# Edge softmax on one core: blocks taken from the fewest slots to the most, and a second turn that follows its block's first turn by two or three steps

## The chip, the core and the metric

The kernel runs on one core of a Trainium2 chip. The metric is the device time of one execution in microseconds (us). The unchanged kernel took 7273.15 us in the median of three runs (7250.3, 7273.15 and 7337.22 us).

## What is computed

A graph of 6250 nodes and 200,000 edges passes through four layers. Each layer adds its result to x after a layer normalisation and a ReLU. The change lies in the third layer, an edge softmax in which every edge has 256 logits and 256 messages:

```python
w_m = (efeat @ W_msg + b_msg).reshape(E, 16, 16)
w_a = (efeat @ W_attn + b_attn).reshape(E, 16, 16)
h_src = feat[src][:, :, None]
e1, e2 = w_m * h_src, w_a * h_src
seg_max = segment_max(e2, dst)
ex = exp(e2 - seg_max[dst])
attn = ex / segment_sum(ex, dst)[dst]
ft = segment_sum(e1 * attn, dst)
return ft.sum(axis=1)          # one row of 16 for each node
```

So a node's maximum over all of its edges has to be known before the first exponential of that node is taken.

## The kernel before

**Blocks, slots, groups.** The nodes are sorted by their number of edges and cut into 49 blocks of 128, one node on each partition. Block b has HELD[b] slots, one edge of each of its nodes in every slot. HELD falls from 64 for block 0 to 21 for block 48 and sums to 1611. Slots are worked on in groups of four (the last group of a block may be shorter). There are 421 groups: 16 in block 0, 12 in block 1, 11 in block 2, down to 6 in block 48.

**Two turns.** Each group is handled twice in `softmax_ranked`.

- The first turn takes the attention logits from TensorE (`logits`, matmuls of L1037 into the PSUM tile `pw`). VectorE multiplies them with the source node's features into `e2` (L1058) and takes a maximum for each partition into `tops` (L1060). After the last group of a block, `less` (L1064) is the negative maximum of the block.
- The second turn asks TensorE for the message logits (again L1037, another `pw` buffer). ScalarE takes exp(e2 + less) into half of the tile `both` (L1069). VectorE multiplies the message logits with the features (L1074) and with the exponentials into the other half (L1075). TensorE adds the group's slots up with identity matmuls into the PSUM tile `acc` (L1083), one of 512 columns for each slot. After the last group, ScalarE copies `acc` out (L1086), and VectorE divides and reduces (L1088 to L1092).

**Steps.** A loop over t writes out all of this by hand: the matmuls for step t+1, `first_take` for step t, the exponential for step t+1, `second_take` for step t and `second_sum` for step t-1. Two lists say which group is in its first turn (`ones`) and which in its second turn (`twos`). The blocks come in the order 0, 1, ..., 48, and `twos` is `ones` shifted by LAG:

```python
LAG = len(groups(0)) // 2 * 2 + 1            # 17
HS = LAG + 1 + len(groups(1)) + len(groups(2))   # 41
ones = [g for b in range(NT) for g in groups(b)]
twos = [None] * LAG + ones + [None]
```

So there are 438 steps: 17 with a first turn alone, 404 with both, 17 with a second turn alone. An odd shift puts the first and the second turn of a step into different halves of the partitions that hold the transposed attributes, and the matmuls of the two halves are issued alternately.

**What is loaded.** `load(b)` puts three kinds of work into the queue of POOL (GpSimd), which works in order. One indirect DMA brings the block's edge attributes (`attr`, L693, three buffers). One indirect DMA for every slot brings 16 features of the slot's 128 source nodes (`hs`, L1007, a tile for each group, HS buffers). A block's result goes out with another indirect DMA (`store`, L51). A tile `hs` is in use from its gather until L1074 of the group's second turn has read it. An `attr` tile is free again when `turn` has copied the block's last pair of groups out of it: ScalarE spreads the attributes (L1018, L1019), TensorE transposes them (L1022), ScalarE copies them to `turned` (L1024). The scheduler of the language orders the instructions within each engine's queue, and can place the attribute load of a block before or behind gathers of other blocks.

**Buffers that bear on the order.** `pw` has three PSUM buffers, `both` four, `e2` LAG + 2 = 19, `turned` LAG // 2 + 7 = 15, `tops` and `less` six, `acc` one.

Of the kernel before, what the change touches and what calls it, by code (L numbers as in the profile page):

```python
# [34 lines left out]
def at(ap):  # L35
    return bass.IndirectOffsetOnAxis(ap=ap, axis=0)
# [914 lines left out]
def softmax_ranked(tc, inp, S, R, dram, x, h):  # L951
# [4 lines left out]
    D, NT = R.D, R.NT  # L956
# [3 lines left out]
    with tc.tile_pool(name="f1", bufs=1) as f1, tc.tile_pool(name="f2", bufs=2) as f2, \  # L960
# [17 lines left out]
        def groups(b):  # L978
            return [(b, s0, min(4, HELD[b] - s0)) for s0 in range(0, HELD[b], 4)]

        def place(b, s0):

            return divmod(s0 + shift[b], 8)

        shift = [4 * (sum(len(groups(i)) for i in range(b)) % 2) for b in range(NT)]

        def chunks(b):
            return place(b, HELD[b] - 1)[0] + 1
# [4 lines left out]
        out = f1.tile([P, NT, D], F32, name="out")  # L993
        state = {}
        LAG = len(groups(0)) // 2 * 2 + 1
        HS = LAG + 1 + len(groups(1)) + len(groups(2))

        def load(b):
            n = HELD[b]
            attr = f2.tile([P, K, D], F32, name="attr", bufs=3)  # L1000
            R.block(attr[:, :n, :].rearrange("p k d -> p (k d)"), inp["edge_attr_16"], b)
            state["attr", b] = attr
            for _, s0, m in groups(b):
                hs = f2.tile([P, 4, D], F32, name="hs", bufs=HS)
                for k in range(m):
                    s = R.base[b] + s0 + k
                    nc.gpsimd.indirect_dma_start(out=hs[:, k, :], out_offset=None, in_=table, in_offset=at(R.src_i[:, s:s + 1]))  # L1007
                state["h", b, s0] = hs

        def turn(b, c):  # L1010

            n, attr, t = HELD[b], state["attr", b], wide[c % 2]
            s0 = 8 * c - shift[b]
            for q in range(2):
                i = [i for i in range(4) if 0 <= s0 + 2 * i + q < n]
                if i:
                    a, z = s0 + 2 * i[0] + q, s0 + 2 * i[-1] + q + 1
                    nc.scalar.copy(t[:, q, i[0]:i[-1] + 1, :D], attr[:, a:z:2, :])  # L1018
                    nc.scalar.copy(t[:, q, i[0]:i[-1] + 1, PAD], R.empty[:, R.base[b] + a:R.base[b] + z:2])  # L1019
            pt = fp.tile([P, 2, P], F32, name="pt")  # L1020
            for q in range(2):
                nc.tensor.transpose(pt[:, q, :], t[:, q].rearrange("p k w -> p (k w)"), S["ident"])  # L1022
            turned = f2.tile([P, 2, P], F32, name="turned", bufs=LAG // 2 + 7)
            nc.scalar.copy(turned, pt)  # L1024
            state["turned", b, c] = turned
# [23 lines left out]
        def ask(first, second):  # L1049
            asked = [(*what, k) for k, what in enumerate((first, second)) if what]  # L1050
            for (b, s0, _, k), pw in zip(asked, logits(*asked)):
                state["am"[k], b, s0] = pw

        def first_take(b, s0, m):
            e2 = f2.tile([P, 4, C], F32, name="e2", bufs=LAG + 2)
            if s0 == 0:
                state["tops", b] = f2.tile([P, K // 4], F32, name="tops", bufs=6)
            nc.vector.tensor_mul(four(e2[:, :m, :]), four(state.pop(("a", b, s0))[:, :m, :]), by_h(b, s0, m))  # L1058
            tops = state["tops", b]
            nc.vector.tensor_reduce(tops[:, s0 // 4:s0 // 4 + 1], e2[:, :m, :], axis=AX.XY, op=OP.max)  # L1060
            state["e2", b, s0] = e2
            if s0 + m == HELD[b]:
                less = f2.tile([P, 1], F32, name="less", bufs=6)
                nc.vector.tensor_reduce(less, tops[:, :s0 // 4 + 1], axis=AX.X, op=OP.max, negate=True)  # L1064
                state["less", b] = less

        def second_exp(b, s0, m):
            both = f2.tile([P, 4, 2 * C], F32, name="both", bufs=4)
            nc.scalar.activation(both[:, :m, :C], state.pop(("e2", b, s0))[:, :m, :], AF.Exp, bias=state["less", b])  # L1069
            state["both", b, s0] = both  # L1070

        def second_take(b, s0, m):
            both, pm = state["both", b, s0], state.pop(("m", b, s0))
            nc.vector.tensor_mul(four(pm[:, :m, :]), four(pm[:, :m, :]), by_h(b, s0, m))  # L1074
            nc.vector.tensor_mul(both[:, :m, C:], pm[:, :m, :], both[:, :m, :C])  # L1075

        def second_sum(b, s0, m):
            if s0 == 0:
                state["acc", b] = fp.tile([P, 2 * C], F32, name="acc")
            acc, both = state["acc", b], state.pop(("both", b, s0))  # L1080
            n = HELD[b]
            for k in range(m):
                nc.tensor.matmul(acc, S["ident"], both[:, k, :], start=s0 + k == 0, stop=s0 + k == n - 1)  # L1083
            if s0 + m == n:
                sums = f2.tile([P, 2 * C], F32, name="sums")
                nc.scalar.copy(sums, acc)  # L1086
                q = f2.tile([P, C], F32, name="q")
                nc.vector.tensor_scalar(q, sums[:, :C], 1.0e-30, None, op0=OP.max, op1=OP.min, accum_out=low[:, b:b + 1])  # L1088
                nc.vector.reciprocal(q, q)
                nc.vector.tensor_mul(q, sums[:, C:], q)  # L1090
                nc.vector.tensor_reduce(out[:, b, :], q.rearrange("p (i o) -> p o i", o=D), axis=AX.X, op=OP.add)
                nc.vector.tensor_scalar(out[:, b, :], out[:, b, :], R.some[:, b:b + 1], None, op0=OP.mult)  # L1092

        def store(b):
            by_node.store(ft, R.node_i[:, b:b + 1], out[:, b, :])

        ones = [g for b in range(NT) for g in groups(b)]
        twos = [None] * LAG + ones + [None]
        ones = ones + [None] * (LAG + 1)
        loaded = turned = stored = 0  # L1100
        todo = [(b, c) for b in range(NT) for c in range(chunks(b))]
        where = {bc: k for k, bc in enumerate(todo)}
        for t in range(-1, len(ones) - 1):
            now, late = (ones[t], twos[t]) if t >= 0 else (None, None)
            if ones[t + 1]:
                b, s0, _ = ones[t + 1]
                while loaded < min(b + 2, NT):
                    load(loaded)
                    loaded += 1
                    if loaded > 6:  # L1110
                        store(stored)
                        stored += 1
                while turned < min(where[b, place(b, s0)[0]] + 2, len(todo)):
                    turn(*todo[turned])
                    turned += 1
            ask(ones[t + 1], twos[t + 1])
            if now:
                first_take(*now)
            if twos[t + 1]:
                second_exp(*twos[t + 1])  # L1120
            if late:
                second_take(*late)
            if t >= 1 and twos[t - 1]:
                second_sum(*twos[t - 1])
        second_sum(*twos[len(ones) - 2])
        while stored < NT:
            store(stored)
            stored += 1
        by_node.done(R.cell)
    with tc.tile_pool(name="f3", bufs=1) as f3:  # L1130
# [276 lines left out]
def gnn(ctx: ExitStack, tc: tile.TileContext, inp, out):  # L1407
# [188 lines left out]
    with tc.If(odd == 0):  # L1596
        with tc.tile_pool(name="fast", bufs=1) as fast:
            dense = Dense(tc, inp, out, S, dram)
            ranked = Ranked(tc, inp, S, fast, dram)
            with tc.tile_pool(name="early", bufs=1) as early:  # L1600
                ranked.scatter()
                with tc.tile_pool(name="slots", bufs=1) as sl:
                    mean_of_edges(tc, inp, S, S["x"], S["h"], lambda b: dense.gather(sl, b))
                    dense.prepare(early)
                ranked.build(early)
                with tc.tile_pool(name="d2", bufs=2) as d2, tc.tile_pool(name="dp", bufs=3, space=PSUM) as dp, \
                        tc.tile_pool(name="dv", bufs=1, space=PSUM) as dv:
                    pieces = dense.build(d2, dp, dv)
                    rational_message(tc, inp, S, ranked, dram, S["x"], S["h"], lambda: next(pieces, None))
                    for _ in pieces:  # L1610
                        pass
            softmax_ranked(tc, inp, S, ranked, dram, S["x"], S["h"])
            dense.wrong = fast.tile([P, 1], F32, name="wrong")
            dense.convolve(S["x"], S["h"])
            ranked.vanishes(fast, dense.wrong, S["odd"])
# [24 lines left out]
```

## Time and profile before

| what | value |
|---|---|
| runs | 7250.3, 7273.15, 7337.22 us |
| profiled execution, its own time | 7443.48 us |
| its span, first to last instruction | 7441.7 us |
| share of the span in which PE, DVE, ACT, POOL are busy | 69%, 57%, 18%, 50% |
| granted clock of TensorE, mean | 0.85 |
| softmax stage: first attribute load to last `out` (L1092) | 3776 to 6777 us |

The profiled execution is 2.3% slower than the median of the runs. All times below are of that execution, and are counted from the start of its span.

A row of a group names the line, the engine, the operation, what it writes and reads, the number of instructions, then the busy time and the mean time of one, then the idle time of the engine just before them with what ended most of it. "remote" and "issue" are waits for which the profile names no instruction. In a table of windows each engine has its busy time and the number of its instructions in that stretch, and PEclk is the clock that TensorE was granted. In a timeline each row has the start, the time, the engine, the line and the tiles, and in brackets the idle time of the engine just before.

### The profile page before, as it was taken

The numbers are of one execution on the slowest core, as the hardware profiler recorded it, in microseconds if no ns is written. First come the engines' busy times: TensorE is split into PE (matmuls) and PEld (weight loads), VectorE is DVE, ScalarE is ACT, GpSimd is POOL, SyncE is SP. The second block draws the span as 40 slices with busy tenths as digits, with TensorE's granted clock in tenths as the row PEclk, the third lists the DMA queues.
The fourth block names the chain that finished last, engine by engine and source line by source line (L and its number), as shares of the span: only waits on it lengthen the run. The fifth ranks groups of instructions, "written<-read, shape, count | busy, mean of one in ns | idle before, by whom it ended". The sixth has DMA issues, their size and how long they took to land.

```text
span 7441.7 us, 69771 instructions
## 1 busy us (share of the span) xinstructions
PE 5142.0 (69%) x26293; PEld 2696.5 (36%) x26293; DVE 4245.6 (57%) x6282; ACT 1337.5 (18%) x2912; POOL 3693.8 (50%) x3729
## 2 busy tenths in 40 slices
PE   0002376767685686777724888888878888898999
PEld 0000144434443344444411334344333334343544
DVE  3753255645564565665523677677667767784211
ACT  0000022212221222222101222222222222220000
POOL 4657654654555555555355555555555555520000
PEclk9997688877787788888856888888888888899999
DMA  2411000000000000001010000000000000004843
GB/s 34 144 14 5 6 22 22 14 22 21 14 22 22 13 22 22 22 14 26 4 18 9 11 10 9 10 10 10 11 10 11 9 9 10 10 4 153 270 148 90
DMA packets 264161, 243.52 MB, mean 33 GB/s; under 512 B 128033, under 2 KB 249819, under 8 KB 260291
## 3 DMA queue, kind: packets, MB, share of 16 engines
q1 hardware_dynamic: 140630, 168.04, 7.8%
q0 software_dynamic: 123184, 70.93, 6.5%
q8 instruction: 209, 3.42, 0.2%
q14 instruction: 138, 1.13, 0.1%
HBM read 195.57 MB, written 43.14 MB: 32 GB/s over the span
## 4 chain that ended last, share of the span: by engine, by line
PE 38%; another core or an unknown queue 17%; issue 16%; POOL 12%; DVE 11%; DMA 2%; ACT 1%; SPq 0%; DVEq 0%; POOLq 0%; ACTq 0%
PE acc L905 18%; POOL hs L1007 9%; PE acc L1353 7%; PE acc L1083 6%; PE pa L1268 3%; PE pw L1037 2%; DVE e L1058 2%; DVE pw L1074 1%; DVE both L1075 1%; DVE ohc L898 1%; DVE st L893 1%; POOL raw L693 1%; POOL slots L1163 1%; DMA hs<-h,rk_src 1%
## 5 line engine op out<-in xcount | busy, mean ns | idle before, releaser
L853 POOL DMA_INDIRECT xi<-h,rk_src x1611 | 1748.7, 1085 | 1328.5 <-DVE den L870 831.7
L1007 POOL DMA_INDIRECT hs<-h,rk_src x1611 | 1521.0, 944 | 1091.1 <-DVE pw L1074 553.0
L905 PE MATMUL acc<-ohc,st 128*128 128x392 bf16 x9666 | 1849.3, 349 | 181.0 <-issue 136.4
L1083 PE MATMUL acc<-both,ident 128*128 128x512 f32 x3222 | 1690.2, 672 | 21.1 <-ACT sums L1086 11.9
L905 PEld LDWEIGHTS <-st 128*128 128x128 bf16 x9666 | 989.1, 103 | 930.3 <-issue 338.0
L1058 DVE TENSOR_TENSOR e<-pw,hs 128x1024 f32<-128x1024 f32 (+2 forms) x421 | 492.1, 1169 | 889.4 <-remote 666.1
L1083 PEld LDWEIGHTS acc<-both,ident 128*128 128x128 f32 x3222 | 651.0, 213 | 872.4 <-issue 851.0
L1037 PE MATMUL pw<-w,turned 18*128 18x256 f32 x6444 | 675.1, 449 | 397.6 <-DVE e L1058 361.7
L893 DVE TENSOR_TENSOR st<-ohx,s 128x1024 bf16<-128x1024 bf16 (+5 forms) x666 | 387.4, 636 | 798.7 <-remote 577.6
L1268 PE MATMUL pa<-oh,ol 128*128 128x98 bf16 x3136 | 372.6, 268 | 637.3 <-ACT adj L1271 329.5
L1069 ACT ACTIVATE both<-e,less 128x1024 f32<-128x1024 f32 (+2 forms) x421 | 467.5, 1111 | 1911.2 <-PE acc L1083 822.6
L1037 PEld LDWEIGHTS pw<-w,turned 18*128 18x128 f32 x6444 | 397.5, 205 | 677.6 <-DVE e L1058 408.6
L1271 ACT CAST adj<-pa 128x392 fp8e4<-128x392 f32 x784 | 347.2, 492 | 1626.8 <-remote 910.0
L898 DVE TENSOR_SCALAR ohc<-places,c 128x784 bf16<-128x784 f16 x1611 | 567.3, 417 | 0.0
L1268 PEld LDWEIGHTS <-ol 128*128 128x128 bf16 x3136 | 299.0, 117 | 726.7 <-issue 690.6
L1353 PE MATMUL acc<-adj,g 128*128 128x512 fp8e4 (+1 forms) x2548 | 540.0, 368 | 30.8 <-DVE g L1313 30.8
L1074 DVE TENSOR_TENSOR pw<-pw,hs 128x1024 f32<-128x1024 f32 (+2 forms) x421 | 495.9, 1178 | 75.7 <-PE pw L1037 30.3
L1075 DVE TENSOR_TENSOR both<-pw,both 128x1024 f32<-128x1024 f32 (+2 forms) x421 | 491.8, 1168 | 4.9
L1060 DVE TENSOR_REDUCE tops<-e 128x1 f32<-128x1024 f32 (+2 forms) x421 | 489.0, 1163 | 1.1
L1263 DVE TENSOR_TENSOR ol<-many,lot 128x2048 bf16<-128x2048 bf16 x196 | 238.3, 1216 | 290.2 <-remote 250.4
L1353 PEld LDWEIGHTS <-g 128*128 128x128 bf16 x2548 | 235.8, 98 | 316.4 <-issue 63.8
L890 ACT COPY ohx<-oha 128x1024 bf16<-128x1024 bf16 (+7 forms) x222 | 214.6, 967 | 544.5 <-DVE st L893 216.1
(257 smaller groups left out, 2584.6 us busy)
## 6 DMA issues: line engine op xcount, KB each, us to landing
adj<-adj SPq DMA_DIRECT2D x252, 448.0 KB
adj<-adj SPq DMA_DIRECT2D x24, 1568.0 KB
xi<-h,rk_src POOLq DMA_INDIRECT x1611
hs<-h,rk_src POOLq DMA_INDIRECT x1611
dis_row<-dis_d SPq DMA_DIRECT2D x1, 3136.0 KB
adj<-adj SPq DMA_DIRECT2D x21, 112.0 KB
rk_pairs<-both SPq DMA_DIRECT2D x1, 1562.5 KB
runs<-in_dst,row_i POOLq DMA_INDIRECT x49
```

The source lines that it names most:

```text
L853: nc.gpsimd.indirect_dma_start(out=xi[:, k, :], out_offset=None, in_=table, in_offset=at(R.src_i[:, s:s + 1]))
L898: nc.vector.tensor_scalar(ohc[:, j, :], places, c[:, s0 + j:s0 + j + 1], None, op0=OP.is_equal)
L905: nc.tensor.matmul(o, st[:, k, j].rearrange("p a d -> p (a d)"), ohc[:, j, half * CW // 2:(half + 1) * CW // 2], start=s == 0 and k == 0, ...
L1007: nc.gpsimd.indirect_dma_start(out=hs[:, k, :], out_offset=None, in_=table, in_offset=at(R.src_i[:, s:s + 1]))
L1037: nc.tensor.matmul(pw[:, k, :], state["turned", b, c][r:r + ROWS, q, :], w[r:r + ROWS, what * C:(what + 1) * C], start=True, stop=True)
L1058: nc.vector.tensor_mul(four(e2[:, :m, :]), four(state.pop(("a", b, s0))[:, :m, :]), by_h(b, s0, m))
L1060: nc.vector.tensor_reduce(tops[:, s0 // 4:s0 // 4 + 1], e2[:, :m, :], axis=AX.XY, op=OP.max)
L1074: nc.vector.tensor_mul(four(pm[:, :m, :]), four(pm[:, :m, :]), by_h(b, s0, m))
L1075: nc.vector.tensor_mul(both[:, :m, C:], pm[:, :m, :], both[:, :m, :C])
L1083: nc.tensor.matmul(acc, S["ident"], both[:, k, :], start=s0 + k == 0, stop=s0 + k == n - 1)
L1268: nc.tensor.matmul(ps[:, j].rearrange("p h w -> p (h w)"), ol[:, b, :, j], oh[:, b, :, j], start=True, stop=True)
L1353: nc.tensor.matmul(acc[i][:, :cols], g3[:, h0 + k, r:r + P], adj[:, :, k, :], start=h0 + k == 0, stop=False)
```

## The change

The blocks are taken from 48 to 0, so from 21 slots to 64. The second turn of a block begins at the first step that is at least two behind the last first turn of the block, is not before the end of the second turn of the block before it, and keeps the distance between the two turns of a group odd. The pool of `hs` tiles grows from 41 to 46, since HS now counts the groups of blocks 0 and 1. LAG stays at 17 and still sets the buffers of `e2` and `turned`. Loads, transposes and stores follow the new order.

```diff
+        order = list(range(NT))[::-1]
+        shift = [4 * (sum(len(groups(i)) for i in range(b + 1, NT)) % 2) for b in range(NT)]
...
-        HS = LAG + 1 + len(groups(1)) + len(groups(2))
+        HS = LAG + 1 + len(groups(0)) + len(groups(1))
...
-        ones = [g for b in range(NT) for g in groups(b)]
-        twos = [None] * LAG + ones + [None]
-        ones = ones + [None] * (LAG + 1)
+        ones, twos = [g for b in order for g in groups(b)], []
+        ends, k = {}, -1
+        for b in order:
+            k += len(groups(b))
+            ends[b] = k
+        for n, b in enumerate(order):
+            t = max(len(twos), ends[b] + 2)
+            t += (t - ends[b] + len(groups(b))) % 2
+            twos += [None] * (t - len(twos)) + groups(b)
+        ones += [None] * (len(twos) + 1 - len(ones))
+        twos += [None]
...
-        todo = [(b, c) for b in range(NT) for c in range(chunks(b))]
+        todo = [(b, c) for b in order for c in range(chunks(b))]
...
-                while loaded < min(b + 2, NT):
-                    load(loaded)
+                while loaded < min(order.index(b) + 2, NT):
+                    load(order[loaded])
                     loaded += 1
                     if loaded > 6:
-                        store(stored)
+                        store(order[stored])
                         stored += 1
```

What the new lists hold can be counted from HELD. There are again 438 steps. 16 have a first turn alone: seven at the start, two before the second turn of each of three blocks (the first one of 25 slots, the first one of 33, the one of 42), and three before that of block 0. One step is empty, 405 have both turns and 16 a second turn alone. The distance between the turns of a group is 7 in the first three blocks, then 9, then 11, then 13, and 17 in block 0.

More of the change, by code (lines that the diff above doesn't have):

```diff
@@ L983, in place @@
             return divmod(s0 + shift[b], 8)
-        shift = [4 * (sum(len(groups(i)) for i in range(b)) % 2) for b in range(NT)]
+        order = list(range(NT))[::-1]
+        shift = [4 * (sum(len(groups(i)) for i in range(b + 1, NT)) % 2) for b in range(NT)]
         def chunks(b):
@@ L1126, in softmax_ranked @@
         while stored < NT:
-            store(stored)
+            store(order[stored])
             stored += 1
```

## The prediction

> **What bounds the kernel now.** I read four views of the softmax stage: the groups, the windows of L1058 alone (one instruction for each first turn, so its count is a count of steps), the windows of all engines, and the timeline of the start. The groups of the page first:
>
> ```profile
> L1007 POOL DMA_INDIRECT hs<-h,rk_src x1611 | 1521.0, 944 | 1091.1 <-DVE pw L1074 553.0
> L1058 DVE TENSOR_TENSOR e<-pw,hs 128x1024 f32<-128x1024 f32 (+2 forms) x421 | 492.1, 1169 | 889.4 <-remote 666.1
> ```
>
> A gather takes 944 ns, and 0.30 us pass before the next one (timeline below), so a group of four costs POOL 5.0 us. POOL lost 553 us waiting for L1074 of some second turn to free a `hs` tile: the gathers are as far ahead as their 41 tiles let them be. Yet L1058 lost 889 us in front of it, mostly to something that the profile calls remote. Both sides wait. The windows of L1058 alone (us, busy time and count, granted clock, DMA share, GB/s):
>
> ```profile
> 3785.00:3820.00 35.00, 6.12 (x5) 0.50 0.07 6
> 3820.00:4007.00 187.00, 8.58 (x8) 0.50 0.09 8
> 4007.00:4027.00 20.00, 7.21 (x6) 0.50 0.00 0
> 4027.00:4084.00 57.00, 10.99 (x10) 0.82 0.08 12
> 4084.00:6575.00 2491.00, 432.03 (x370) 0.86 0.08 10
> 6575.00:6690.00 115.00, 27.15 (x24) 0.97 0.01 3
> ```
>
> With gathers under way a step costs 2491 / 370 = 6.73 us. After the last gather (6575 us) 24 first turns and 41 second turns remain and take until 6773 us: 198 / 41 = 4.83 us a step. The first 17 steps, which have only a first turn, take 3785 to 4027 = 242 us, 14.2 us each, although they have less to do: five go at the usual pace, eight take 187 us, and the last six come within 20 us, once the gathers have stopped (DMA share 0.00). All engines (PE, PEld, DVE, ACT, POOL):
>
> ```profile
> 4084.00:6575.00 2491.00, 2082.35 (x8916) 976.30 (x8913) 1762.46 (x1776) 576.90 (x1383) 1418.76 (x1500) 0.86 0.08 10
> 6575.00:6690.00 115.00, 112.26 (x533) 53.55 (x532) 107.60 (x117) 35.58 (x87) 3.92 (x5) 0.97 0.01 3
> ```
>
> After the last gather PE is full (112 of 115 us): 4.83 us is PE's own pace. Before it PE is busy 2082 / 370 = 5.63 us a step at a lower clock, and the other 1.1 us are waits. Now the start:
>
> ```profile
> 3828.08 2.10 PE L1037 MATMUL pw<-w,turned 18*128 18x256 f32 x16
> ...
> 3846.55 0.94 POOL L1007 DMA_INDIRECT hs<-h,rk_src  x1 [0.31 <-issue]
> 3847.80 0.94 POOL L1007 DMA_INDIRECT hs<-h,rk_src  x1 [0.30 <-issue]
> 3848.04 1.23 DVE L1058 TENSOR_TENSOR e<-pw,hs 128x1024 f32<-128x1024 f32 x1 [24.51 <-issue]
> ...
> 4028.36 0.94 POOL L1007 DMA_INDIRECT hs<-h,rk_src  x1 [42.32 <-DVE pw L1074]
> ```
>
> The gathers follow each other without a gap from 3785 to 3987 us. PE's 16 matmuls for the logits end at 3830, but VectorE goes on only at 3848, and again only at 3876: 28 us for a step of 5 us, with its gathers landed long before. From 3987 POOL stands for 42.3 us, all tiles full, and the waiting steps come out in a rush from about 4007, 20 us after the last gather. So what one engine has finished reaches the next one late while gathers run unbroken, and about 20 us of lateness are piled up at the end of such a run. In the steady part the runs are short (553 / 138 = 4.0 us of pause each), so the loss is small.
>
> **The change, step by step.** The sum is made in the profiled execution (span 7441.7 us, its own time 7443.48), which is 2.3% above the median of 7273.15; I scale the difference by 7273 / 7443 = 0.977.
>
> (1) *What is as before.* The instructions of every engine are the same in kind and number (1611 gathers, 421 of each step's operations, 49 attribute loads and stores). There are 438 steps again: 17 alone, 404 both, 17 alone become 16, 405, 16 and one empty. So nothing is won by work; only places move.
>
> (2) *The gathers' lead.* A group's tile is free after its second turn, so POOL leads by HS less the distance less 1: 41 - 18 = 23 groups now, 46 - 8, 10, 12, 14 = 38 to 32 after. Steady pace is not set by the lead: POOL is at its limit now and will be at it again, and runs and pauses alternate as before. I keep 6.73 us. Bounds: 5.63 (PE's busy time, the waits gone) and, if the runs between pauses get longer, more than 6.73; the nearest row, 6.73, has the same limit in force, so I take it. A quarter of the way to 5.63 would be 0.28 x 360 = 99 us less, about where rival A ends; the low end of the range reaches there.
>
> (3) *The start.* Seven steps alone instead of 17. By count that saves 10 x 14.2 = 142 us. But the eight slow steps are slow because of the gathers' unbroken run, and that run is not shorter: in the order of POOL the attribute load of the seventh block, which waits for `turn` of the fourth block's last slots (behind the first-turn logits of group 21 on PE), stands behind 163 gathers; now 165 gathers fill the tiles. Behind that waiting load stand the gathers of all later groups; nobody needs them soon, the lead being 20 groups. 163 gathers and six attribute loads end near 3995 us. Until then first turns 0 to 5 go as before (to 3820), one or two alone at 28 us, then steps with both turns, at 28 us or more each since PE's results are late for both turns: first turn 10 by about 4015 (20 us of lateness included). Then nine steps at 4.83 us bring group 19 by 4058 and free the load. POOL, with some 13 tiles empty, makes a second run of about 65 us: 5 steps before lateness builds up, the rest at about 28 us. Group 27, reached at 4084 us now, comes at about 4155: **+71 us**. Low end: if only what is in the first run counts, +19; high end +110, if steps with both turns take twice 28 us.
>
> The Trainium skill speaks against the second run costing more than this in another way: "TensorE: Matmul & The Clock Gate", Part 1 (the HAM clock gate), says that TensorE falls to half clock after an idle window. The rows agree on the clock (0.50 until 4027), and the sums of a group took 6.02 us at the half and 3.70 us at the full clock, 2.3 us more. By the rule ten steps with both turns, moved into the cold start, cost 10 x 2.3 x 2 (logits and sums) = 46 us on top; by the rows these lie inside the 28 us of lateness of a step. I take nothing, and 46 us as part of the high end.
>
> (4) *The stretch with gathers.* Now 370 steps from first turn 27 to the last gather, 370 x 6.73 = 2490. After: the last group's tile is that of group 374, freed at step 387, so the gathers end 10 steps earlier: 356 steps at 6.73 and 4 alone at 5.0 = 2416: **-74 us**.
>
> (5) *Behind the last gather.* Now 41 steps, 198 us. After, 51 steps are left: 46 x 4.83 + 3 lone first turns x 2.4 (half of a step) + 4 us for the chain at block 0 = 233: **+35 us**.
>
> (6) *Block boundaries.* The first exponential of a block now stands one step behind `less` (before, 17 steps). ScalarE does it in 1.11 us, with a whole VectorE step of four operations (1.17 + 1.16 + 1.18 + 1.17 = 4.7 us) as cover. I take 0; if the cover is gone it costs one chain (rival B). A wait there would hold ScalarE's copies of `turned`, which are two pieces ahead.
>
> A second rule is weighed here: "SBUF — State Buffer", "SBUF: two separate sides", has DMA and engine ports disjoint, so that transfers cannot slow computing. By it a step with gathers would cost the longer of 5.0 and 4.83 us, and (4) and (5) would be 10 x 0.2 = -2 us. The row says 6.73; the trace decides, whatever the path is by which gathers delay the others.
>
> Sum: +71 - 74 + 35 = +32 us profiled, +31 on the median: **7305 us**. With 19 in place of 71, or 110 and half of the 46, and one per cent of (4), 24 us, either way: -44 to +118 profiled, 7230 to 7390.
>
> **Rivals.** *A, the start shrinks with its count.* If the lateness falls on each lone step, not on the gathers' run: -142 - 74 + 35 = -181 profiled, -177: 7096 us. For it: 14.2 us is the dearest step of the stage. Against it: six of the 17 came within 20 us without gathers.
>
> *B, slower: the boundary starves VectorE.* One step of cover is 4.7 us, but the longest waits of L1058 reach 10.6 us in the stretch with gathers, so `less` or the exponential can be late by more than its cover. If the chain of 1.17 + 1.16 + 0.15 + 1.11 + 1.18 + 1.17 = 5.9 us lies open at each of 48 boundaries: 283 us, with the other terms about +250 when part of it lies in waits that are there anyway: 7520 us. From (145 - 31) / 48 = 2.4 us a boundary it is slower by over 2%. For it: ScalarE's exponential is late behind others' operations already. Against it: it mostly waits for a free `both`, thus it is early.
>
> *C, nothing moves.* The gathers' path sets a total that is the same for 1611 gathers wherever they stand: 7273 us. For it: equal work; against it: pace with and without gathers is different, and ten steps change sides.
>
> **How the numbers follow.** Main case 0.43, A 0.20, B 0.22, C 0.15. The likeliest one's time is 7305 us, its own range 7230 to 7390. Two per cent is 145 us, about what a measurement of this kernel can tell from no change. Faster by over that: 0.15 of A and 0.02 of the main case, 0.17. Slower: 0.19 of B and 0.04 of the main case, 0.23. Within: 0.60. The range, 7100 to 7480, cuts off about half of A and the upper part of B, 0.1 each.
>
> **What would show it.** In the profile after: L1058's 28th instruction near 4155 us (A: near 3950); a long pause of POOL in front of an attribute load near 3995; the gathers 32 to 38 groups ahead; 6.7 us a step until the last gather, then 51 steps at 4.8. B would show as a wait of L1075 or of the exponential on `less` at every sixth to ninth step. The forecast fails most easily at the start, since no row shows steps with both turns in a long unbroken run, and in (2), if a longer lead changes how runs and pauses alternate.

## The result and the profile after

| | before | after |
|---|---|---|
| median of 20 runs, us | 7273.5 (7183.35 to 7337.22) | 7356.59 (7300.22 to 7441.93) |
| ratio after / before | | 1.0126 (95%: 1.010 to 1.015) |
| profiled execution, its span, us | 7441.7 | 7379.0 |
| first gather to last L1074 (after: L1075), us | 2979 | 2994 |

The change costs 83 us by the medians, about 1.1%. The ratio of 1.0126 leaves out the runs of a kernel that are more than 1.5% above its fastest one; either way the cost is under 2%, and the interval lies above 1. The forecast was 7305 us (+31) with a range of 7100 to 7480: the sign was right, the size too small. The two profiled spans stand the other way round: the profile of before is 168 us above the median of its runs, the one of after only 22, and before is 82 us later already where the softmax stage begins (first gather at 3785 us, after at 3704). So the two spans are not subtracted here; the parts of the stage are compared.

The line numbers of the changed kernel are one higher. The two groups of its page that answer to those shown of before:

```profile
L1008 POOL DMA_INDIRECT hs<-h,rk_src x1611 | 1522.2, 945 | 950.8 <-issue 452.4
L1059 DVE TENSOR_TENSOR e<-pw,hs 128x1024 f32<-128x1024 f32 (+2 forms) x421 | 492.2, 1169 | 819.2 <-remote 633.1
```

The gathers take as long as before, and the first turns still wait mostly for what the profile calls remote. The windows of L1059 alone, in the changed kernel (same columns as before: us, busy time and count, clock, DMA share, GB/s):

```profile
3704.00:3738.00 34.00, 6.54 (x6) 0.50 0.11 13
3738.00:3935.00 197.00, 4.90 (x4) 0.53 0.08 8
3935.00:3985.00 50.00, 11.94 (x10) 0.85 0.03 6
3985.00:4051.00 66.00, 1.22 (x1) 0.62 0.07 6
4051.00:4105.30 54.30, 6.52 (x6) 0.74 0.06 9
4105.30:6477.00 2371.70, 423.39 (x362) 0.87 0.08 10
6477.00:6627.00 150.00, 37.00 (x32) 1.00 0.01 1
```

Six quick steps, then four first turns in 197 us; ten come in 50 us when the gathers pause, then one in 66 us. From the first gather to first turn 27 it takes 4105 - 3704 = 401 us, where before took 4084 - 3785 = 299. The timeline shows both halves of this (changed kernel; L1059, and the one attribute load that POOL waits for):

```profile
3762.24 1.23 DVE L1059 TENSOR_TENSOR e<-pw,hs 128x1024 f32<-128x1024 f32 x1 [25.41 <-remote]
3812.63 1.22 DVE L1059 TENSOR_TENSOR e<-pw,hs 128x1024 f32<-128x1024 f32 x1 [49.11 <-issue]
3857.43 1.23 DVE L1059 TENSOR_TENSOR e<-pw,hs 128x1024 f32<-128x1024 f32 x1 [32.37 <-remote]
3907.84 1.23 DVE L1059 TENSOR_TENSOR e<-pw,hs 128x1024 f32<-128x1024 f32 x1 [37.97 <-remote]
3976.54 0.94 POOL L693 DMA_INDIRECT attr<-in_edge_attr,rk_start  x1 [66.94 <-ACT wide L1020]
4010.34 1.22 DVE L1059 TENSOR_TENSOR e<-pw,hs 128x1024 f32<-128x1024 f32 x1 [22.56 <-remote]
4052.37 1.22 DVE L1059 TENSOR_TENSOR e<-pw,hs 128x1024 f32<-128x1024 f32 x1 [11.89 <-remote]
```

First turns are counted from 0. The lone ones of before came mostly 22 to 34 us apart in the unbroken run. Steps with both turns in the same place come 45 to 50 us apart (3762, 3813, 3857, 3908). At 3910 POOL stops for 66.9 us at the attribute load that needs the fourth block's last slots, behind 163 gathers as forecast; then it starts a second run, in which first turn 21 comes 42 us behind 20. Of the 103 us, 31 are lost up to first turn 19, where the first run ends, and 72 in the eight steps behind it. All engines of the changed kernel, in the first run, in the stretch with gathers and behind the last gather:

```profile
3735.00:3935.00 200.00, 27.14 (x92) 13.34 (x92) 18.47 (x18) 11.36 (x31) 132.17 (x140) 0.53 0.08 8
4105.30:6477.00 2371.70, 2012.94 (x8633) 950.68 (x8634) 1717.54 (x1735) 569.10 (x1438) 1376.70 (x1455) 0.87 0.08 10
6477.00:6627.00 150.00, 149.30 (x756) 71.87 (x754) 141.21 (x140) 43.78 (x106) 2.66 (x3) 1.00 0.01 1
```

In the first run PE is busy for 27 of 200 us. Behind the last gather it is full (149.3 of 150 us), as before.

### The profile page after: what moved, and what is told of

It is laid out like the page before. It is cut to its first block, busy times and chain, and to the rows that moved or that the text cites. A ratio compares the mean times of both kernels' runs of the same rounds, so it can differ in the third digit from the quotient of the medians.

```text
span 7379.0 us, 69815 instructions
## 1 busy us (share of the span) xinstructions
PE 5157.0 (70%) x26333; PEld 2707.2 (37%) x26333; DVE 4248.7 (58%) x6282; ACT 1349.5 (18%) x3000; POOL 3684.1 (50%) x3729
## 4 chain that ended last, share of the span: by engine, by line
PE 41%; another core or an unknown queue 16%; DVE 14%; issue 14%; POOL 8%; DMA 2%; ACT 1%; DVEq 0%; SPq 0%; POOLq 0%; ACTq 0%
PE acc L905 18%; PE acc L1084 9%; PE acc L1364 7%; POOL hs L1008 5%; PE pw L1038 3%; PE pa L1279 3%; DVE e L1059 3%; DVE pw L1075 2%; DVE both L1076 2%; DVE ohc L898 1%; DVE st L893 1%; POOL xi L853 1%; DVE tops L1061 1%; POOL raw L693 1%
## 5 line engine op out<-in xcount | busy, mean ns | idle before, releaser
L1059 DVE TENSOR_TENSOR e<-pw,hs 128x1024 f32<-128x1024 f32 (+2 forms) x421 | 492.2, 1169 | 819.2 <-remote 633.1
L1075 DVE TENSOR_TENSOR pw<-pw,hs 128x1024 f32<-128x1024 f32 (+2 forms) x421 | 495.8, 1178 | 144.1 <-PE pw L1038 63.7
```

## The experiments

The runs fell into two kinds. On two chips the kernel before takes 5952 to 5968 us, on two others 7241 to 7344 us, as in the result above. I call them quick and late chips. One chip was used twice, and was quick both times; whether a chip always stays of its kind was not seen. Every ratio is to the kernel before on the same chip, with its 95% interval. Most of the later expectations state a case for each kind. What the runs gave, with the parts of the stage counted from the first gather:

| kernel | chip | time, us | ratio | first turn 27 | last gather | behind it | us a step between |
|---|---|---|---|---|---|---|---|
| before, first profile | late | 7273.5 | | 299 | 2791 | 189 | 6.74 |
| changed, first profile | late | 7356.6 | 1.0126 (1.010 to 1.015) | 401 | 2774 | 220 | 6.55 |
| before_again | quick | 5964.8 | 1 (one run) | 141 | 2125 | 115 | 5.15 |
| after_again | quick | 5950.5 | 0.9998 (0.999 to 1.001) | 156 | 2130 | 112 | 5.14 |
| order_only, order_only_b | quick | 5933.3, 5922.5 | 0.9941, 0.9935 (0.992 to 0.996) | 148 | 2128 | 77 | 5.04 |
| after_s24, after_s24b | quick | 5937.8, 5918.3 | 0.9946, 0.9926 (0.991 to 0.997) | 184 | 2131 | 73 | 4.95 |
| after_closed2 | quick | 6584.0 | 1.104 (1.101 to 1.107) | 145 | 2778 | 74 | 6.70 |
| paced24 | quick | 6767.3 | 1.135 (1.133 to 1.137) | 155 | 2978 | 78 | 7.20 |
| before_s24 | late | 7255.8 | 0.986 (0.980 to 0.992) | 213 | 2760 | 106 | 6.58 |
| after_attr | late | 7419.5 | 1.0097 (1.007 to 1.013) | 399 | 2789 | 219 | 6.60 |
| best30 | late | 7323.6 | 0.997 (0.9945 to 0.9995) | 268 | 2786 | 140 | 6.75 |
| after_s20 | late | 7218.9 | 0.998 (0.995 to 1.0005) | 236 | 2769 | 94 | 6.53 |

The last column divides the time from first turn 27 to the last gather by the first turns in it. In best30 four steps of that stretch have a second turn alone, so it has 377 steps of 6.68 us.

**The kernel before again (before_again).** No edit.

> The kernel before, unchanged, for a second profile of it: the first one was 7443 us long where 20 runs have a median of 7273.5. My theory (the change costs about 100 us at the start and gives part of it back later): of the missing 170 us some 80 lie ahead of the softmax stage, and the stage from the first hs gather to the last L1074, 2980 us in the first profile, comes to about 2900; the first 27 groups take about 300 us again. Rival (the change costs nothing at the start and something at each block): the start of the first profile was itself an outlier, and the first 27 groups take near 400 us here.

It ran on a quick chip, so what it was meant to settle stays open: the pace of before on a late chip in an execution near its median. It showed something else. Windows of L1058 in this profile, and one line of its timeline:

```profile
3046.00:3136.00 90.00, 20.81 (x17) 0.50 0.09 7
3136.00:5171.00 2035.00, 460.08 (x395) 0.97 0.09 13
```

```profile
3087.14 1.22 DVE L1058 TENSOR_TENSOR e<-pw,hs 128x1024 f32<-128x1024 f32 x1 [3.77 <-DMA hs<-h,rk_src]
```

The same gathers, issued without a pause, delay nobody here: at the same half clock (0.50) 17 lone first turns take 90 us (242 on the late chip), the first turn shown waits only for its own group's gathers, and later a step takes 2035 / 395 = 5.15 us at a clock of 0.97. That is close to the 5.0 us that POOL needs for a group, so here the gathers set the pace.

**The changed kernel on a quick chip (after_again).** No edit.

> The changed kernel, unchanged, since in the first four runs the kernel before itself took 5968 us, not 7273, and its first turns came 1.4 us behind their gathers, without any lateness. Theory (the loss comes from lateness that piles up in unbroken gathers, and from nothing else in the change): where the kernel before runs near 5968 us, there is no lateness, the 17 lone steps cost one group's gathers each (5 us), and the change is not slower: a ratio of 0.99 to 1.0, as order alone and 24 tiles alone had (0.994). Where the kernel before runs near 7270 us the ratio is 1.01 again. Rival (the short distance leaves the exponential or less late at each of 48 blocks): slower at both speeds, 1.01 or more here too.

0.9998: neither faster nor slower. The shorter start does what its count says: the first second turn comes 41 us after the first gather, not 94. But the gain is given back (windows of L1059, then all engines in the last of these windows, then the wait of ACT):

```profile
3061.00:3258.50 197.50, 37.94 (x34) 0.85 0.08 10
3258.50:3331.00 72.50, 2.26 (x2) 0.56 0.08 10
3331.00:5150.00 1819.00, 429.45 (x368) 0.98 0.09 14
```

```profile
3331.00:5150.00 1819.00, 1777.35 (x8840) 856.43 (x8841) 1739.53 (x1765) 582.81 (x1479) 1376.39 (x1453) 0.98 0.09 14
```

```profile
3329.55 0.24 ACT L1019 COPY wide<-attr 128x64 f32<-128x64 f32 x1 [75.82 <-DMA attr<-in_edge_attr,rk_start]
```

ScalarE waits 75.8 us for the eighth block's attributes, whose load stands behind 240 gathers in POOL's queue, and with it the matmuls and all steps stand. The gathers go on meanwhile, so their end does not move (2130 us after the first one, 2125 before); but the steps, now behind the gathers, catch up only in part, and the stage ends with 112 us of them behind the last gather, as it did before (115). While they catch up, over most of the block boundaries, PE is busy for 1777 of 1819 us. So the boundary theory (dearer on both kinds) is out: hardly any time is left for waits at a boundary.

**The order alone (order_only, order_only_b).** The blocks from 48 to 0, the old rule and size:

```diff
-        ones, twos = [g for b in order for g in groups(b)], []
-        ends, k = {}, -1
...
+        ones = [g for b in order for g in groups(b)]
+        twos = [None] * LAG + ones + [None]
+        ones = ones + [None] * (LAG + 1)
...
-        HS = LAG + 1 + len(groups(0)) + len(groups(1))
+        HS = LAG + 1 + len(groups(1)) + len(groups(2))
```

> The blocks from 48 to 0, but the second turn a constant 17 steps behind the first, and 41 hs tiles. If the loss comes from steps with both turns inside the first unbroken run of gathers, these are lone steps again and the first 27 groups take about 300 us: 7273 us, within 30. If it comes from the short distance at block boundaries, the distance is 17 again: 7273 too. If the order of the blocks itself costs (short blocks first, and the attribute loads with them), it stays near 7357.

> The blocks from 48 to 0 with a constant distance of 17 and 41 tiles once more, if this time the kernel before runs near 7300 us. My theory: the steps in the first unbroken run are lone again, 28 us each and not 50, and the run breaks off at an attribute load behind 144 gathers: m=0 near 220 us after the first gather, group 27 near 290 us, 0.99 to 1.00 of the kernel before. Rival (the order of the blocks is what costs): 1.01.

Both runs came on quick chips, so on a late chip the order alone was not measured. On a quick one it wins 0.6%. ScalarE waits long for attributes here too, but earlier in the stage:

```profile
3178.07 0.63 ACT L1019 COPY wide<-attr 128x32 f32<-128x32 f32 x4 [58.34 <-DMA attr<-in_edge_attr,rk_start]
```

The pieces that it had copied before carry the steps over: no two first turns are more than 23 us apart, where after_again had a hole of 75. 77 us are left behind the last gather.

**Fewer hs tiles (after_s24, after_s24b, before_s24, after_s20).** Gathers written group by group, as many ahead as there are tiles:

```diff
-        HS = LAG + 1 + len(groups(0)) + len(groups(1))
+        HS = 24
...
+            while gathered < min(HS + free, 421):
+                gather(*ones[gathered])
+                gathered += 1
             ask(ones[t + 1], twos[t + 1])
...
                 second_take(*late)
+                free += 1
```

after_s20 has 20 in place of 24; before_s24 is the same edit of the kernel before.

> The changed kernel with 24 hs tiles in place of 46, the gathers written group by group as tiles come free. Theory of the start: the first run of gathers ends after 24 groups (about 120 us, not 205), group 27 comes about 265 us after the first gather, not 401; 29 steps in place of 51 are left behind the last gather, 22 x 1.8 = 39 us dearer: about 7260 us. Rival, the stock of gathered groups keeps the steps fed: with 10 to 16 groups of lead the steps wait for gathers, more than 7400 us. Rival, the loss is at the block boundaries: 7357, no change.

> The changed kernel with 24 hs tiles once more, if this time the kernel before runs near 7300 us (near 5960 it had 0.9946 and would have it again). My theory: the first run of gathers ends after 24 groups, so group 27 comes about 265 us after the first gather, not 401, and fewer steps (29) are left behind the last gather, 39 us dearer: 97 us less than the changed kernel, 0.999 of the kernel before. Rival (the loss is not in the first runs but in the distance or the boundaries): 1.0126 as the changed kernel.

> The kernel before with 24 hs tiles in place of 41, the gathers written group by group as tiles come free. Where the kernel before runs near 7270 us (late results in long runs of gathers): the first run ends after 24 groups, not 41, the first 27 groups come 76 us earlier, 25 steps in place of 41 are left behind the last gather and cost 30 us more: 0.994 of the kernel before. Where it runs near 5960 us (no lateness): the gathers set the pace and end at the same time whatever the lead, and the 17 lone second turns of 4.5 us are all that is left: 76 us in place of 115: 0.9935. Rival (a stock of gathered groups is worth something by itself): 1.00 or more at both.

> The changed kernel with 20 hs tiles, the gathers written group by group. Where the kernel before runs near 7300 us: the first unbroken run is 20 groups (some 95 us), so by my theory only first turns 6 and 7 fall into it and group 27 comes about 240 us after the first gather, not 400; the steps behind the last gather go from 51 to about 25 and cost 45 us more: 115 us less than the changed kernel, 0.997 of the kernel before. Rival (distance or boundaries cost, not the first runs): 1.0126 as the changed kernel; rival (so little lead starves the steps): 1.02 or more. Where the kernel before runs near 5960 us: as with 24 tiles, 0.993 to 0.995.

On the quick chips the 24 tiles have 73 us behind the last gather and 0.993 to 0.995, the same as the order alone with its constant distance of 17: the short distance at 48 boundaries costs nothing that can be seen. They stop for attributes as well, for 49 us at first turn 21, and have caught up by the end: this wait is shorter and comes earlier than that of after_again. The size of the expectation for after_s24 (7260) was for a late chip; on a quick one neither of its rivals shows: steps did not starve with 24 tiles, and nothing was lost at the boundaries. On late chips before_s24 shows what the length of the first run costs. Windows of its L1059:

```profile
3708.00:3748.00 40.00, 7.35 (x6) 0.50 0.15 27
3748.00:3834.00 86.00, 3.67 (x3) 0.50 0.10 7
3834.00:3868.00 34.00, 10.67 (x9) 0.50 0.00 0
3925.00:6472.00 2547.00, 451.40 (x386) 0.88 0.08 10
```

Three slow steps instead of eight, then nine in 34 us once POOL's tiles are full (DMA share 0.00). First turn 27 comes 213 us after the first gather, not 299. That is 86 us (expected 76), and behind the last gather there are 106 us, not 189. The whole came out better than expected, 0.986 for 0.994; why was not found. The changed kernel with 20 tiles lost nearly all of its deficit: 0.998 (expected 0.997). Windows of its L1060:

```profile
3668.00:3700.00 32.00, 6.55 (x6) 0.50 0.11 13
3700.00:3770.00 70.00, 1.23 (x1) 0.50 0.07 6
3770.00:3904.50 134.50, 23.25 (x21) 0.82 0.08 11
3904.50:6437.00 2532.50, 454.37 (x388) 0.88 0.08 10
```

One slow step, and first turn 27 at 236 us (expected 240), where the changed kernel had 401. Same order, same distances, same boundaries: what is taken away is the length of the first runs and most of the lead. From the first gather to the last L1074 the two kernels with few tiles take the same time (before_s24 2866 us, after_s20 2863). Their ratios were taken on two chips, where the kernel before took 7344 and 7241 us, so which of them is better stays open.

**An earlier place for the attribute loads (after_attr).** `bufs=3` of `attr` becomes `bufs=5`.

> The changed kernel with five attr tiles in place of three, so that the attribute loads stand earlier in POOL's queue. In the run of the changed kernel at 5950 us the eighth block's load stood behind 240 gathers, and all engines waited for it for 75 us at group 42, after the shorter start had won 53 us. Without that wait, where the kernel before runs near 5960: the last gather at about the same time, 16 lone second turns behind it, 73 us in place of 111: 0.9935 of the kernel before. Where it runs near 7270: POOL no longer stops after 163 gathers and the first unbroken run gets longer, 184 gathers: 1.01 to 1.02. Rival (the 75 us are covered by gathers anyway, and what is left at the end stays): 1.000, as the changed kernel.

1.0097 on a late chip, its interval overlapping that of the change, and first turn 27 comes at 399 us. The pause only moved: POOL goes past the attribute load, but stops at the first store of a block (L51, 56.7 us, after 170 gathers, not the 184 expected), and 16 first turns, not 18, are done when it goes on. So this run does not tell what a start without the pause would take. Its use on a quick chip was not tried.

**The old order with a falling distance (best30).** 30 tiles, gathers as above, and:

```diff
-        twos = [None] * LAG + ones + [None]
-        ones = ones + [None] * (LAG + 1)
+        parts, twos, ones = ones, [None] * LAG + ones + [None], [None] * (len(ones) + LAG + 1)
+        for j, g in enumerate(parts):
+            ones[LAG + j - (len(groups(g[0])) // 2 * 2 + 1 + len(groups(g[0])) % 2 * 2)] = g
```

> The old order, 64 slots first, and 30 hs tiles; each block's second turn two or three steps behind its own first one, so the distance falls from 17 to 7 (steps with a second turn alone come in between), and only 7 lone second turns are left at the end. Where the kernel before runs near 5960: gathers end at the same time, then about 9 steps of 4.5 us, 40 us in place of 115: 0.988. Where it runs near 7270: a first run of 30 groups instead of 41, the start 40 us shorter, the same 438 steps, some 20 fewer of them behind the last gather and 1.9 us dearer: 1.00. Rival (the lead at the end is worth what it costs): 1.00 at both.

0.997 on a late chip: first turn 27 at 268 us, some 30 earlier than in the profile of before (40 expected). The shorter run helps; before_s24, with 24 tiles and the constant distance, has 0.986, so the falling distance gained nothing there that would make up for six more tiles.

**Gathers held back (after_closed2, paced24).** POOL copies each group's offsets into one of two small tiles first, which waits for the gathers of two groups earlier; paced24 (kernel before, 24 tiles, four such tiles) also fills a tile of 128x512 in front of each group:

```diff
+                ids = f2.tile([P, 4], mybir.dt.int32, name="ids", bufs=2)
...
+                nc.gpsimd.tensor_copy(ids[:, :m], R.src_i[:, s:s + m])
...
-                    ... in_offset=at(R.src_i[:, s:s + 1])
+                    ... in_offset=at(ids[:, k:k + 1])
```

> The changed kernel, but the offsets of each group's gathers are first copied by POOL into one of two small tiles, so that a group's gathers cannot be issued before those of two groups earlier are done. If the loss is lateness that piles up because POOL issues gathers faster (1.25 us) than something behind it serves them, at most 8 are ever open and nothing piles up: group 27 within 250 us of the first gather, steps in the stretch with gathers near 5.6 us, 6900 to 7150 us in all. If gathers slow the others by what each one moves, whenever it is issued, the start stays near 400 us, and POOL's waits come on top: 7357 to 7600 us.

> The kernel before with 24 hs tiles, and in front of each group's gathers POOL first fills a tile of 128x512 and copies the offsets into it: some 0.8 us more, so a gather about every 1.45 us, not 1.25. Where the kernel before runs near 7300 us: if the lateness is a queue that grows because gathers are issued faster than something serves them (about 1.4 us each by the late start), it no longer grows: lone steps at 5.8 us, not 28, steps of both turns near 5.9, not 6.6, 0.94 to 0.96 of the kernel before. Rival (each gather delays the others by a fixed amount however it is spaced): as 24 tiles alone, 0.986, or slower by POOL's extra work, up to 1.02. Where the kernel before runs near 5960 the gathers alone set the pace, and 421 x 0.8 us come on top less what the shorter end saves: 1.045.

Both ran on quick chips, where there is no lateness to remove, so neither tells of it. paced24 missed its size there too (1.135 for 1.045). POOL's fill waits for a gather to land; by the time it is the one just before it, although there are four of the small tiles (timeline of paced24):

```profile
4002.28 0.94 POOL L1011 DMA_INDIRECT hs<-h,ids  x1 [0.30 <-issue]
4004.72 0.53 POOL L1008 MEMSET ids<- 128x512 int32 x1 [1.49 <-DMA hs<-h,ids]
4005.31 0.19 POOL L1009 COPY ids<-rk_src 128x4 int32<-128x4 int32 x1
```

1.49 + 0.53 + 0.19 us make a group 7.2 us, not 5.8. Whether evenly spaced gathers would stop the lateness on a late chip was not tried.

## Why the prediction was right, and where its sizes were off

**(1) The same work.** Right: 0.9998 where the gathers set the pace.

**(2) Lead and pace.** The lead was as forecast: at second turns 40 and 370 the gathers were 35 and 34 groups ahead of the first turns (23 and 23 before). 6.73 us a step was kept, 6.55 measured. A long lead is not what makes it quicker: after_s20, with some 7 to 10 groups of lead, has 6.53 and before_s24, with 5 to 6, 6.58, beside 6.60 of after_attr with 33 to 35. The 6.73 was read in an execution 168 us above its median, and best30, in the old order and near its median, has 6.68. Whether before runs nearer to 6.58 in an ordinary execution was not seen. One slip in the bounds: a quarter of the way to 5.63 makes about 7208 us, not where rival A ends (7096).

**(3) The start.** The mechanism was right, the size 32 us short: +103 for +71, inside its high end of 110. First turn 10 was to come 230 us after the first gather and came at 231; first turn 19 at 273, and came at 278. The last eight steps were to take 97 us and took 123. The mis-sized term is the second run, "5 steps before lateness builds up, the rest at about 28 us". Lateness was there at once: the first two steps of the run took 28 and 42 us, a later one 25, the other five 28 together. In the first run a step of both turns took 45 to 50. The half clock (0.53 in that window) was there, as the rule of the Trainium skill that the prediction cites has it ("TensorE: Matmul & The Clock Gate", Part 1), but it explains little: PE was busy for 27 of those 200 us, and at the full clock it would have saved at most half of that. The quick chip shows the same: 17 first turns in 90 us at 0.50. (The counts 5, 8 and 6 of the prediction make 19, not 17: one instruction lies in two windows, and one belongs to the first step with both turns. Nothing rests on it.)

**(4) and (5) The stretch and the end.** The stretch was to be 74 us shorter and is 120 by the two profiles. Behind the last gather 49 steps were left, near the 51 of the forecast: 45 with a second turn, three with a first turn alone, and the empty one. By the table they took 31 us more than before (+35 expected). So the parts of the two profiles make 103 - 120 + 31 = +14 us, where the medians say +83. Part of the 168 us by which the profile of before is above its median must then lie in this stage; its pace is the likeliest place, but that is argued. With 6.58 for both kernels the stretch would save 53 us and the sum be +81; with the 6.68 of best30 for before it would be about +34. So the start's loss is measured, but how much of it the stretch gives back stays open, and that the whole came out inside the narrower range of 7230 to 7390 is in part luck.

**(6) Boundaries.** Right: nothing that can be seen. On quick chips the short distance is as fast as 17, and on late ones after_s20 has the pace of before_s24.

**The rivals.** A (the start shrinks with its count) is what happens on a quick chip, 94 to 41 us, but not where gathers make the others late. B (boundaries) fell. C (nothing moves) is the result on a quick chip.

The rule that the Trainium skill gives in "SBUF — State Buffer", "SBUF: two separate sides", was set aside for the row of 6.73. On the quick chips steps take 4.95 to 5.15 us, close to the 5.0 that the rule's reading gave; on late chips 6.5 to 6.7. The forecast held for the kind of chip that its profile came from. The profile alone did not show that there is another.

**Shown:** the loss is in the start, is there only on late chips, and goes when fewer tiles cut the runs of gathers short (after_s20: 236 us for 401, 0.998 for 1.0126). **Argued from the profiles:** that a step of both turns in such a run costs 42 to 50 us where a lone one costs about 28. The run that changes this alone, the order with a constant distance of 17, never came on a late chip. **Open:** what in a late chip delays the engines' results. Not the gathered data: where POOL pauses behind a gather, its last packet lands about 1 us behind POOL's instruction on both kinds (median 1.11 us in before, 1.04 in before_again).

**A version that beats before on a late chip.** before_s24, 7255.8 us (four runs) beside 7344.3 on its chip: 0.986, so by less than 2%. On quick chips it was not run; the changed kernel with 24 tiles has 0.9926 and 0.9946 there.

## What to carry to other kernels

A deep stock of prefetched tiles need not be free: while it was being filled here, the queue ran without a pause, and on late chips the steps beside it were late; try the smallest number of tiles that keeps the consumer fed. A load that one step needs soon must not stand behind a hundred that nobody needs yet. When a stretch of the profile holds waits without a named releaser, find out whether another chip shows them too, before a schedule is built around them.

## What was not expected of the hardware

The same kernel took about 5960 us on two chips and 7240 to 7340 on others. POOL's and VectorE's instructions in this layer took the same (a gather 945 ns, a first turn's multiplication 1.17 us). TensorE was busy for 5142 us in the late profile and 4789 in the quick one, at mean clocks of 0.85 and 0.935; of the 1480 us between the two that is about 350, and most of the rest is waits: L1058 idled 889 us in the late profile, mostly for "remote", and 114 us in the quick one. Even ahead of the softmax stage the quick chip was 3785 - 3046 = 739 us earlier. On the late chips the engines' results reached one another late while gathers ran; in the profiles of the quick ones no such wait shows.
